# Attention scores of layer 1: the 64-row group taken in two turns of 32 rows

## The chip, the cores and the metric

The kernel runs on one core of a Trainium2 chip. The metric is the device time of one execution, in microseconds. TensorE is called PE (its weight loads PEld), VectorE DVE, ScalarE ACT, GpSimd POOL, and SyncE, which issues most of the DMAs, SP.

## The reference

The program has two layers on an input of 4 x 32 x 128 x 128. Layer 0, a Fourier layer with attention, is not touched. Layer 1 normalizes each token of 128 channels and runs causal additive attention over the 4096 tokens of each of four sequences, then a mixture of eight experts of which each token takes two:

```python
f = jnp.einsum('bih,ha->bia', x, W1[:h])
g = jnp.einsum('bjh,ha->bja', x, W1[h:])
t = jnp.tanh(f[:, :, None, :] + g[:, None, :, :] + b1)
scores = jnp.einsum('bija,a->bij', t, w2[:, 0]) + b2[0]
flag = jnp.tril(jnp.ones((n_seq, n_seq), dtype=x.dtype), -1)[None, :, :]
e = jnp.exp(scores) * flag
denom = jnp.sum(e, axis=-1, keepdims=True) + 1e-10
w = e / denom
return jnp.einsum('bij,bjh->bih', w, x)
```

The score is a sum of 16 terms w2[a] tanh(f + g + b1[a]). All arithmetic is fp32.

## The kernel before

**The scores as products.** A sum of tanh terms over m hidden units can be written as a quotient n / d, where d is a sum over the 2**m patterns of signs of exp(sign sum of the query) times exp(sign sum of the key), and n is the same sum with each pattern weighted by its signed sum of w2. Both are matrix products of a key matrix and a query matrix with 2**m rows. The 16 hidden units are cut into groups of 6, 5 and 5 (`GROUP_SIZES`), so the groups have 64, 32 and 32 rows, 128 together; `_signs` builds the patterns side by side. The score is the sum of the three quotients.

**Keys and queries.** `prepare` makes a chunk of 1024 tokens (`IC`): normalize, transpose, one product each with `mk` and `mq`, then an Exp on ACT. That gives `ke` and `qe` on 128 rows. `ks` is `ke` times the signed sums of w2. `exchange` copies a tile to another with its upper and lower 64 rows swapped, by two DMAs on SP: `kf` from `ks`, `qf` from `qe`. So d is made from `ke` and `qe`, with group 0 on rows 0 to 63 and the others on 64 to 95 and 96 to 127; n is made from `kf` and `qf`, with group 0 on rows 64 to 127 and the others on 0 to 31 and 32 to 63. The helper pieces that do this (`as_keys`, `as_queries`) and those of the expert layer (`attention`, `transpose_half`, `first`, `experts`) are lists of small steps with estimated costs on DVE and POOL; the loop hands out at most one PE piece per unit.

**Units.** A unit is a block of 128 keys against 512 queries (`QC`); there are 528. Units on the diagonal hold two parts of fewer columns. The order is written out by hand (`manual_schedule`), in a loop of stages over u:

- `products(u)` (L1282) on PE: the three products d of unit u and the three products n of unit u-1. They are sorted so that the four products of groups 1 and 2 (32 rows each, on four different row tiles) come first, and then the two of group 0 (64 rows each).
- ACT, L1335: Ln of d into `r`, in two instructions, one on the bank pair of groups 1 and 2 (1024 columns), one on the bank of group 0 (512).
- DVE, L1340: `r` of unit u-1 times n, in the same two parts; then POOL, L1343 and L1344, adds the three groups into `e`, the first two being groups 0 and 1.
- ACT, L1347: Exp of -`r` of unit u (1536 columns), which turns Ln d into 1/d. ACT, L1351: Exp of the score `e` of unit u-2. On diagonal blocks POOL multiplies with the mask `later` (L1356).
- `attend(u-4)` (L1301) on PE: `e` times the normalized tokens `kx`, summed in the bank `po`.
- Then pieces of the other work, above all `experts` (`px`, L1180, with four sums on DVE each, L1184).

**Banks.** The PSUM pool of layer 1 has one buffer per tile. `two_parts` gives d and n a tile of two banks each (`d0`, `n0`: groups 1 and 2) and a tile of one bank each (`d1`, `n1`: group 0); `po` and the pieces' tile `m` have the last two. PE can write a tile of unit u+1 only when ACT (d) or DVE (n) has read that of the unit before.

Of the kernel before, what the change touches and what calls it, by code (L numbers as in the profile page):

```python
# [9 lines left out]
ALU = mybir.AluOpType  # L10
# [3 lines left out]
P = 128  # L14
# [64 lines left out]
def _signs():  # L79


    groups = []
    a = 0
    for m in GROUP_SIZES:
        s = np.zeros((A + 1, 2**m), np.float32)
        for n in range(2**m):
            for i in range(m):
                s[a + i, n] = -1.0 if n >> i & 1 else 1.0
        groups.append(s)
        a += m  # L90
    groups[0][A] = 1.0
    return np.concatenate(groups, 1)


def _inv_std(nc, small, out, var, eps, nhalf):
# [814 lines left out]
def layer1(tc, x1, w1t_in, signs, vec17, expert_w, expert_b, router_w, small_row, out):  # L910
    nc = tc.nc
# [25 lines left out]
        out=later,  # L937
        in_=later,
# [17 lines left out]
    def misc(name):  # L956
# [9 lines left out]
        out=eb.rearrange("p e c -> p (e c)"),  # L966
        in_=expert_b.rearrange("e c -> (e c)").partition_broadcast(P),
    )
    for w, row in (
# [4 lines left out]
        n = w.shape[1]  # L974
# [87 lines left out]
    def prepare(b, i0, own, beside):  # L1062

        kx, ke, kf = own
        xc = work.tile([P, NB, C], F32, name="xc", tag="xc", bufs=4)
        nc.sync.dma_start(out=xc, in_=x1[b, i0 : i0 + NB].rearrange("t w c -> w t c"))
        own_kx = kx[:, i0 : i0 + NB]
        xt = work.tile([P, IC], F32, name="xt", tag="xt", bufs=1)  # L1070
        qe, qf = (work.tile([P, IC], F32, name=n, tag=n, bufs=3) for n in ("qe", "qf"))

        def exchange(dst, src):
            nc.sync.dma_start(out=dst[:64], in_=src[64:])
            nc.sync.dma_start(out=dst[64:], in_=src[:64])

        def as_keys(h):
            i = slice(i0 * P + h * 512, i0 * P + (h + 1) * 512)
            pz = misc("pz")
            nc.tensor.matmul(pz, mk, xt[:, h * 512 : (h + 1) * 512], start=True, stop=True)  # L1080
            nc.scalar.activation(ke[:, i], pz, AF.Exp, bias=kbias)
            ks = work.tile([P, 512], F32, name="ks", tag="ks", bufs=1)
            nc.gpsimd.tensor_scalar(ks, ke[:, i], kmul, None, ALU.mult)
            exchange(kf[:, i], ks)

        def as_queries(h):
            i = slice(h * 512, (h + 1) * 512)
            pz = misc("pz")
            nc.tensor.matmul(pz, mq, xt[:, i], start=True, stop=True)
            nc.scalar.activation(qe[:, i], pz, AF.Exp, bias=qbias)  # L1090
            exchange(qf[:, i], qe[:, i])

        load = [(NONE, 0.0, 0.0, lambda: None), gap] * 2
        sums, after = norm_pieces(xc, own_kx, NB, beside)
        pieces = [(SOME, 0.7, 0.0, lambda h=h: transpose_half(own_kx, xt, h)) for h in range(2)]
        for h in range(2):
            pieces.append((SOME, 0.0, 1.6, lambda h=h: as_keys(h)))
            pieces.append((SOME, 0.0, 0.0, lambda h=h: as_queries(h)))
        return (qe, qf), load + sums + after, pieces
# [125 lines left out]
    state = {}  # L1225
    sums = {}
    live = {}

    def begin(c, beside=True):
# [9 lines left out]
        state[c] = (own, qs)  # L1239
        return norm, pieces  # L1240

    def operands(u, part):


        c, _, _, parts = units[u]
        k, q = state[c][0][1 + part], state[c][1][part]
        for g, r0, n in ((0, 0, 64), (1, 64, 32), (2, 96, 32)):
            r0 = (r0 + 64 * part) % P
            for n_part, (jb, h, q0, c0, c1) in enumerate(parts):
                j = slice(jb * P, (jb + 1) * P)  # L1250
                i = h * QC + q0
                yield g, n_part, c0, c1, k[r0 : r0 + n, j], q[r0 : r0 + n, i : i + c1 - c0]

    PARTS = slice(1, 3), slice(0, 1)

    def two_parts(name):
        return [
            ps.tile([P, g.stop - g.start, 512], F32, name=f"{name}{k}", tag=f"{name}{k}")  # L1260
            for k, g in enumerate(PARTS)
        ]

    def groups_of(parts):
        return parts[1][:, 0], parts[0][:, 0], parts[0][:, 1]

    def products(u):

        todo = []
        if u < len(units):  # L1270
            live[u, "d"] = two_parts("d")
            dst = groups_of(live[u, "d"])
            todo += [(dst[g][:, c0:c1], g, p, k, q) for g, p, c0, c1, k, q in operands(u, 0)]
        if 0 <= u - 1 < len(units):
            live[u - 1, "n"] = two_parts("n")
            dst_n = groups_of(live[u - 1, "n"])
            todo += [
                (dst_n[g][:, c0:c1], g, p, k, q) for g, p, c0, c1, k, q in operands(u - 1, 1)
            ]

        for o, _, _, k, q in sorted(todo, key=lambda t: (t[1] == 0, t[2])):
            nc.tensor.matmul(o, k, q, start=True, stop=True)  # L1282

    kept = []

# [35 lines left out]
    norm_1, todo = begin(1, beside=False)  # L1321
# [6 lines left out]
    with tc.manual_schedule():  # L1328
        for u in range(len(units) + 4):
            products(u)  # L1330
            if u < len(units):
                r = work.tile([P, 3, QC], F32, name="r", tag="r", bufs=3)
                live[u, "r"] = r
                for g, d in zip(PARTS, live.pop((u, "d"))):
                    nc.scalar.activation(r[:, g], d, AF.Ln, scale=1.0 / DSCALE)  # L1335
            if 0 <= u - 1 < len(units):
                v = u - 1
                r, n = live.pop((v, "r")), live.pop((v, "n"))
                for g, part in zip(PARTS, n):
                    nc.vector.tensor_tensor(r[:, g], part, r[:, g], ALU.mult)  # L1340
                e = work.tile([P, QC], F32, name="e", tag="e", bufs=5)
                live[v, "e"] = e
                nc.gpsimd.tensor_tensor(e, r[:, 0], r[:, 1], ALU.add)  # L1343
                nc.gpsimd.tensor_tensor(e, e, r[:, 2], ALU.add)  # L1344
            if u < len(units):
                r = live[u, "r"]
                nc.scalar.activation(r, r, AF.Exp, scale=-1.0)  # L1347
            if 0 <= u - 2 < len(units):
                c, h, _, parts = units[u - 2]
                e = live[u - 2, "e"]  # L1350
                nc.scalar.activation(e, e, AF.Exp)  # L1351
                if parts[0][0] >= chunks[c][1] + h * QB:

                    width = 2 * P if parts[-1][1] != h else P
                    own = e[:, : len(parts) * width].rearrange("p (k c) -> p k c", c=width)[:, :, :P]
                    nc.gpsimd.tensor_tensor(own, own, later[:, : len(parts)], ALU.mult)  # L1356
            if 0 <= u - 4 < len(units):
                attend(u - 4)
                c, h, is_last, _ = units[u - 4]
                if is_last and c == len(chunks) - 1:  # L1360
                    b, i0 = chunks[c]
                    ending.append((b, i0 + h * QB, QB, [sums[c, h]]))
                elif is_last and h == 1:
                    ending.append((*chunks[c], NB, [sums[c, h] for h in range(2)]))

            if starts and u >= starts[0][0] and not todo:
                _, c, end = starts.pop(0)
                todo = sum(begin(c), [])
            if ending and (not ended or len(ended) == 1 and len(ended[0]) <= 2 * NB):
                ended.append(finish(*ending.pop(0)))  # L1370
            hurry = sum(p[0] in (SOME, LATER) for p in todo) + 6 > end - u
            queues = sorted(ended, key=lambda p: len(p) <= 2 * NB)
            queues.insert(0 if hurry else 2, todo)
            pe, dve, pool = False, 0.0, 0.0
            for pieces in queues:
                while pieces:
                    kind, t_dve, t_pool, piece = pieces[0]
                    if kind == LATER:
                        pieces.pop(0)
                        break  # L1380
                    if kind and pe or dve + t_dve > 1.8 or pool and pool + t_pool > 1.7:
                        break
                    if kind in (SOME, KEEPS) and keeper and keeper[0] is not pieces:
                        break
                    pe, dve, pool = pe or kind > 0, dve + t_dve, pool + t_pool
                    if kind in (KEEPS, KEPT):
                        keeper = [pieces] if kind == KEEPS else []
                    pieces.pop(0)
                    piece()
            ended = [p for p in ended if p]  # L1390
# [80 lines left out]
```

## Time and profile before

| | |
|---|---|
| median of 3 runs | 3289.89 us (3287.66 to 3298.04) |
| profiled execution | 3282.17 us, span 3280.4 us, TensorE clock granted 0.971 |
| layer 1's loop | from about 1151 to 3219 us of the span |
| DVE product L1340, 1024 columns | 1.22 us mean; 512 columns 0.68 us |
| POOL add L1343 or L1344 | 1.27 us |
| Exp L1351 | 0.62 us |

The page of the profile lists, for each engine, its busy time, share of the span and number of instructions. A line of a group names the source line, engine, operation, output and inputs, shape and count, then the busy time in us and the mean in ns, then the idle time ahead of it and who ended it. A line of the timeline begins with its start in us from the span's start and its duration. An fp32 product is recorded as two weight loads and two matmuls. `32*128` is the tile shape on TensorE, rows by columns.

### The profile page before, as it was taken

Reading aid. Unit: us, or ns where it says so; the run is one execution under the profiler, and the core shown is the slowest. Engines: PE = TensorE matmul, PEld = TensorE weight load, DVE = VectorE, ACT = ScalarE, POOL = GpSimd, SP = SyncE. Lnnn points to the kernel's source line nnn. Section 1 sums busy time; section 2 is a strip of 40 time slices with the busy share of each in tenths; the row PEclk is TensorE's granted clock in tenths of the full one; section 3 lists DMA queues with packets and bytes.
Section 4 is the critical chain, followed back from the end, with each engine's and each line's share of the span. In section 5 each row is a group of like instructions: output and inputs, shape, how many; then the busy total and the mean of one; then the engine's idle time right before and its main releaser. Section 6 shows DMA issues by size and latency. Waiting matters only on the chain.

```text
span 3280.4 us, 48731 instructions
## 1 busy us (share of the span) xinstructions
PE 3065.3 (93%) x17428; PEld 1488.6 (45%) x17428; DVE 2319.8 (71%) x5070; ACT 2356.6 (72%) x3205; POOL 2138.0 (65%) x1883
## 2 busy tenths in 40 slices
PE   6899899899898699999999999999999999999997
PEld 4378368458558533333333333333333334333333
DVE  6766777767677556777666767766777776677777
ACT  2334444354344289999999999998999999999992
POOL 1730641551460279868798787889877879888773
PEclk8999899999999799999999999999999999999998
DMA  4400510330230111010110000011100010101000
GB/s 109 118 21 1 118 51 1 70 99 1 30 113 1 53 39 26 7 26 7 27 33 20 14 20 14 7 26 26 26 23 11 14 33 20 33 1 26 14 13 13
DMA packets 148274, 107.17 MB, mean 33 GB/s; under 512 B 35358, under 2 KB 138881, under 8 KB 147425
## 3 DMA queue, kind: packets, MB, share of 16 engines
q1 hardware_dynamic: 131313, 98.22, 11.7%
q10 hardware_dynamic: 16720, 5.84, 0.8%
q8 instruction: 138, 2.26, 0.3%
q14 instruction: 103, 0.84, 0.1%
HBM read 67.26 MB, written 20.00 MB: 27 GB/s over the span
## 4 chain that ended last, share of the span: by engine, by line
PE 70%; POOL 12%; DVE 7%; ACT 5%; issue 4%; DMA 2%; ACTq 0%; POOLq 0%; DVEq 0%; SPq 0%
PE d L1282 24%; PE po L1301 12%; PE px L1180 6%; PE po L716 4%; PE pz L272 4%; POOL e L1344 3%; POOL e L1343 3%; PE four L294 3%; PE px L280 2%; PE px L279 2%; PE pv L289 2%; ACT r L1335 2%; POOL kx L1044 2%; PE n L1282 2%; PE sk L680 1%
## 5 line engine op out<-in xcount | busy, mean ns | idle before, releaser
L1282 PE MATMUL d<-qe,ke 32*128 32x512 f32 (+7 forms) x3456 | 1166.2, 603 | 20.9 <-ACT r L1335 20.2
L1340 DVE TENSOR_TENSOR r<-n,r 128x1024 f32<-128x1024 f32 (+1 forms) x1056 | 958.6, 949 | 305.3 <-ACT r L1347 189.0
L1282 PE MATMUL n<-qf,kf 32*128 32x512 f32 (+7 forms) x3456 | 1158.5, 602 | 0.0
L1343 POOL TENSOR_TENSOR e<-r 128x512 f32<-128x512 f32 x528 | 671.9, 1273 | 318.0 <-DVE r L1340 275.8
L1335 ACT ACTIVATE r<-d 128x1024 f32<-128x1024 f32 (+1 forms) x1056 | 823.0, 805 | 69.5 <-PE n L1282 58.8
L1347 ACT ACTIVATE r<-r 128x1536 f32<-128x1536 f32 x528 | 783.4, 1484 | 16.8
L1344 POOL TENSOR_TENSOR e<-e,r 128x512 f32<-128x512 f32 x528 | 671.8, 1272 | 41.4
L1282 PEld LDWEIGHTS d<-qe,ke 32*128 32x128 f32 (+1 forms) x3456 | 351.7, 184 | 701.6 <-issue 239.8
L1301 PE MATMUL po<-e,kx 128*128 128x512 f32 (+3 forms) x1152 | 594.3, 604 | 10.1 <-POOL e L1356 10.1
L1184 DVE SCALAR_TENSOR_TENSOR xc<-px,wgt,xc 128x128 f32<-128x128 f32 x1024 | 358.5, 351 | 211.1 <-PE px L1180 178.5
L1351 ACT ACTIVATE e<-e 128x512 f32<-128x512 f32 x528 | 325.9, 617 | 74.3 <-POOL e L1344 73.9
L1282 PEld LDWEIGHTS n<-qf,kf 32*128 32x128 f32 (+1 forms) x3456 | 350.5, 184 | 19.0 <-DVE r L1340 0.9
L1301 PEld LDWEIGHTS po<-e,kx 128*128 128x128 f32 x1152 | 175.4, 188 | 381.5 <-issue 297.2
L711 POOL TENSOR_TENSOR u<-xb,gb 128x858 f32<-128x858 f32 (+1 forms) x120 | 234.7, 1983 | 118.0 <-PE po L716 93.1
L798 POOL TENSOR_TENSOR spec<-spec,part 128x264 f32<-128x264 f32 x64 | 55.3, 865 | 392.6 <-DVE part L795 187.3
L1180 PE MATMUL px<-we,x2t 128*128 128x512 f32 x512 | 266.3, 606 | 7.1 <-DVE xc L1184 6.2
L713 DVE TENSOR_TENSOR u<-xw,gb 128x858 f32<-128x858 f32 (+1 forms) x200 | 206.9, 1084 | 52.9 <-PE po L716 36.8
L716 PE MATMUL po<-u,pr 128*32 128x429 f32 (+1 forms) x1280 | 188.8, 542 | 18.7 <-POOL u L711 9.0
L705 ACT COPY xw<-xb 128x429 f32<-128x429 f32 (+1 forms) x160 | 83.6, 526 | 122.8 <-DVE pa L557 93.2
L1180 PEld LDWEIGHTS px<-we,x2t 128*128 128x128 f32 x512 | 96.6, 194 | 121.2 <-issue 104.5
L217 ACT COPY z<-pz 128x384 f32<-128x384 f32 x127 | 60.7, 478 | 118.9 <-PE pz L272 118.5
L559 POOL TENSOR_TENSOR pb<-xm 128x1024 f32<-128x1024 f32 x48 | 90.6, 1915 | 81.9 <-ACT xm L493 73.8
(365 smaller groups left out, 3911.2 us busy)
## 6 DMA issues: line engine op xcount, KB each, us to landing
xb<-xd SPq DMA_DIRECT2D x128, 214.5 KB
xc<-x SPq DMA_DIRECT2D x31, 512.0 KB
x<-x SPq DMA_DIRECT2D x16, 512.0 KB
kf<-ks SPq DMA_DIRECT2D x64, 128.0 KB
qf<-qe SPq DMA_DIRECT2D x64, 128.0 KB
out<-xc SPq DMA_DIRECT2D x15, 512.0 KB
xb<-xd SPq DMA_DIRECT2D x32, 198.0 KB
gb<-gd SPq DMA_DIRECT2D x4, 1056.0 KB
```

The costliest lines, as they stand in the source:

```text
L711: nc.gpsimd.tensor_tensor(u, xb, gk, ALU.mult)
L716: nc.tensor.matmul(po[32 * j : 32 * j + 32], pr[:, i, k], u[:, r], start=i == 0 and k == 0, stop=i == 3 and k == 1,)
L1180: nc.tensor.matmul(px, x2t[:, k * P : (k + 1) * P], we[:, e0 : e0 + 4], start=True, stop=True)
L1184: nc.vector.scalar_tensor_tensor(xc[:, k], px[:, e], wgt[:, k, e0 + e : e0 + e + 1], xc[:, k], ALU.mult, ALU.add)
L1282: nc.tensor.matmul(o, k, q, start=True, stop=True)
L1301: nc.tensor.matmul(sums[c, h][:, q0 : q0 + c1 - c0], kx[:, jb], e[:, c0:c1], start=jb == 0, stop=is_last and q0 > 2 * P, skip_group_check= ...
L1335: nc.scalar.activation(r[:, g], d, AF.Ln, scale=1.0 / DSCALE)
L1340: nc.vector.tensor_tensor(r[:, g], part, r[:, g], ALU.mult)
L1343: nc.gpsimd.tensor_tensor(e, r[:, 0], r[:, 1], ALU.add)
L1344: nc.gpsimd.tensor_tensor(e, e, r[:, 2], ALU.add)
L1347: nc.scalar.activation(r, r, AF.Exp, scale=-1.0)
L1351: nc.scalar.activation(e, e, AF.Exp)
```

## The change

The group of 64 rows is multiplied as two products of 32 rows that add up in one bank, the first with start, the second with stop. For d, group 0 is on rows 0 to 31 in both turns and the second group of each turn on rows 32 to 63; for n they are on rows 64 to 95 and 96 to 127. Turn 0 reads `ke` and `qe`, turn 1 `kf` and `qf`, so the columns of `_signs` are put in another order and the tiles hold other halves. `ke` and `kf` now carry both the plain and the weighted keys: three copies of half height per half chunk, the last of which overwrites the lower half of `ke`. The six products of a unit become eight, sorted by part and turn. The tile `d0` now holds groups 1 and 0 and `d1` group 2; `n0` holds groups 0 and 2 and `n1` group 1. POOL first adds groups 0 and 2, then group 1.

```diff
-    return np.concatenate(groups, 1)
+    first, second, third = groups
+    return np.concatenate([first[:, :32], second, first[:, 32:], third], 1)
...
-            exchange(kf[:, i], ks)
+            nc.sync.dma_start(out=kf[:64, i], in_=ke[64:, i])
+            nc.sync.dma_start(out=kf[64:, i], in_=ks[:64])
+            nc.sync.dma_start(out=ke[64:, i], in_=ks[64:])
...
-            exchange(qf[:, i], qe[:, i])
+            nc.sync.dma_start(out=qf[:64, i], in_=qe[64:, i])
+            nc.sync.dma_start(out=qf[64:, i], in_=qe[:64, i])
...
+    ROWS = (((0, 0), (1, 32)), ((0, 0), (2, 32))), (((0, 64), (2, 96)), ((0, 64), (1, 96)))
...
-        k, q = state[c][0][1 + part], state[c][1][part]
-        for g, r0, n in ((0, 0, 64), (1, 64, 32), (2, 96, 32)):
-            r0 = (r0 + 64 * part) % P
+        for turn, rows in enumerate(ROWS[part]):
+            q = state[c][1][turn]
             for n_part, (jb, h, q0, c0, c1) in enumerate(parts):
+                k = state[c][0][1 + turn]
                 j = slice(jb * P, (jb + 1) * P)
                 i = h * QC + q0
-                yield g, n_part, c0, c1, k[r0 : r0 + n, j], q[r0 : r0 + n, i : i + c1 - c0]
+                for g, r0 in rows:
+                    r = slice(r0, r0 + 32)
+                    yield g, (n_part, turn), c0, c1, k[r, j], q[r, i : i + c1 - c0]
...
-    PARTS = slice(1, 3), slice(0, 1)
+    PARTS = {"d": (slice(0, 2), slice(2, 3)), "n": (slice(1, 3), slice(0, 1))}
...
-        for o, _, _, k, q in sorted(todo, key=lambda t: (t[1] == 0, t[2])):
-            nc.tensor.matmul(o, k, q, start=True, stop=True)
+        for o, g, (_, turn), k, q in sorted(todo, key=lambda t: t[2]):
+            nc.tensor.matmul(o, k, q, start=turn == 0 or g > 0, stop=turn == 1 or g > 0)
...
-                nc.gpsimd.tensor_tensor(e, r[:, 0], r[:, 1], ALU.add)
-                nc.gpsimd.tensor_tensor(e, e, r[:, 2], ALU.add)
+                nc.gpsimd.tensor_tensor(e, r[:, 1], r[:, 2], ALU.add)
+                nc.gpsimd.tensor_tensor(e, e, r[:, 0], ALU.add)
```

More of the change, by code (lines that the diff above doesn't have):

```diff
@@ L1071, in prepare @@
         qe, qf = (work.tile([P, IC], F32, name=n, tag=n, bufs=3) for n in ("qe", "qf"))
-        def exchange(dst, src):
-            nc.sync.dma_start(out=dst[:64], in_=src[64:])
-            nc.sync.dma_start(out=dst[64:], in_=src[:64])
         def as_keys(h):
@@ L1260, in two_parts, with groups_of @@
             ps.tile([P, g.stop - g.start, 512], F32, name=f"{name}{k}", tag=f"{name}{k}")
-            for k, g in enumerate(PARTS)
+            for k, g in enumerate(PARTS[name])
         ]
-    def groups_of(parts):
-        return parts[1][:, 0], parts[0][:, 0], parts[0][:, 1]
+    def groups_of(name, parts):
+        places = {}
+        for g, t in zip(PARTS[name], parts):
+            for k in range(g.start, g.stop):
+                places[(1, 0, 2)[k]] = t[:, k - g.start]
+        return places
     def products(u):
@@ L1271, in products @@
             live[u, "d"] = two_parts("d")
-            dst = groups_of(live[u, "d"])
+            dst = groups_of("d", live[u, "d"])
             todo += [(dst[g][:, c0:c1], g, p, k, q) for g, p, c0, c1, k, q in operands(u, 0)]
@@ L1275, in products @@
             live[u - 1, "n"] = two_parts("n")
-            dst_n = groups_of(live[u - 1, "n"])
+            dst_n = groups_of("n", live[u - 1, "n"])
             todo += [
@@ L1333, in layer1 @@
                 live[u, "r"] = r
-                for g, d in zip(PARTS, live.pop((u, "d"))):
+                for g, d in zip(PARTS["d"], live.pop((u, "d"))):
                     nc.scalar.activation(r[:, g], d, AF.Ln, scale=1.0 / DSCALE)
@@ L1338, in layer1 @@
                 r, n = live.pop((v, "r")), live.pop((v, "n"))
-                for g, part in zip(PARTS, n):
+                for g, part in zip(PARTS["n"], n):
                     nc.vector.tensor_tensor(r[:, g], part, r[:, g], ALU.mult)
```

## The prediction

> **What bounds the kernel now.** I read the page first: busy times, then the groups.
>
> ```profile
> PE 3065.3 (93%) x17428; PEld 1488.6 (45%) x17428; DVE 2319.8 (71%) x5070; ACT 2356.6 (72%) x3205; POOL 2138.0 (65%) x1883
> ...
> L1335 ACT ACTIVATE r<-d 128x1024 f32<-128x1024 f32 (+1 forms) x1056 | 823.0, 805 | 69.5 <-PE n L1282 58.8
> L1347 ACT ACTIVATE r<-r 128x1536 f32<-128x1536 f32 x528 | 783.4, 1484 | 16.8
> ```
>
> The change lies in layer 1's attention, 528 units (the count of L1347) from about 1151 us. There PE and ACT are both nearly full, so I went to the order of time. First TensorE alone, in a stretch where one unit has an expert matmul (px) and one has none:
>
> ```profile
> 2510.76 0.70 PE L1282 MATMUL d<-qe,ke 32*128 32x512 f32 x2
> 2510.77 0.70 PE L1282 MATMUL n<-qf,kf 32*128 32x512 f32 x2
> 2511.29 0.59 PE L1282 MATMUL d<-qe,ke 32*128 32x512 f32 x2
> ...
> 2511.83 0.69 PE L1282 MATMUL d<-qe,ke 64*128 64x512 f32 x1
> ...
> 2512.89 1.12 PE L1301 MATMUL po<-e,kx 128*128 128x512 f32 x2
> 2513.85 1.02 PE L1180 MATMUL px<-we,x2t 128*128 128x512 f32 x2
> 2514.80 0.70 PE L1282 MATMUL d<-qe,ke 32*128 32x512 f32 x2
> ```
>
> An fp32 product runs as two passes. Read the starts: four 32-row tiles side by side take 1.07 us, the two 64-row tiles take 1.06, po 0.96, px 0.95. They differ though each has two passes of 512 columns. Weight loads explain it:
>
> ```profile
> 2511.83 0.18 PEld L1282 LDWEIGHTS d<-qe,ke 64*128 64x128 f32 x1 [0.76 <-issue]
> ...
> 2512.89 0.30 PEld L1301 LDWEIGHTS po<-e,kx 128*128 128x128 f32 x2 [0.76 <-issue]
> 2513.43 0.19 PEld L1180 LDWEIGHTS px<-we,x2t 128*128 128x128 f32 x1 [0.24 <-issue]
> ```
>
> px has the tile shape of po. Its weights load at 2513.43, during po's second pass, and it starts at 2513.85, 0.42 after that pass began: one pass streams in about 0.427. Where the shape changes (32 to 64 rows, 64 to 128), the load comes only when the old work is out: 1.07 = 2 x 0.427 + 0.107 (load not hidden) + 0.107 (emptying). A change of shape thus costs about 0.21 us.
>
> Does a second turn on the same 32-row tiles get the cheap hand-over? A unit cut in two parts shows it:
>
> ```profile
> 1359.53 0.91 PE L1282 MATMUL n<-qf,kf 32*128 32x384 f32 x4
> ...
> 1360.27 0.39 PE L1282 MATMUL n<-qf,kf 32*128 32x128 f32 x4
> ```
>
> 384 columns, two passes: 0.107 + 2 x 0.320 = 0.747, so 1360.27. The next product on the same tiles starts with no gap.
>
> Then I took the start-to-start time of the 492 units between 1290.5 and 3213.2 us from the timeline and sorted them by what else PE does in them. Mean 3.908. With px: 4.05 in 207 of 227; with the mean-free attention (pa) or a transpose (pt): 3.63 in 89 of 112; key and query products (pz): 4.05 in 42 of 52; router (pl): 4.87 in all 14; nothing else: 3.19 in 57 of 87. These are exactly PE's own sums (1.07 + 1.06 + 0.96 + 0.95 = 4.04), so PE is the bound in most units. The other 70 or so are longer: 3.43 where ACT sets it, 4.1 to 4.8 where POOL does. ACT's case:
>
> ```profile
> 1637.35 0.70 PE L1282 MATMUL d<-qe,ke 32*128 32x512 f32 x2 [0.18 <-ACT r L1335]
> ...
> 1639.72 1.49 ACT L1335 ACTIVATE r<-d 128x1024 f32<-128x1024 f32 x2
> ...
> 1640.78 0.19 PEld L1282 LDWEIGHTS d<-qe,ke 32*128 32x128 f32 x2 [1.00 <-ACT r L1335]
> ```
>
> A unit's ACT work back to back is 3.43 (1.49 + 1.48 + 0.61 less overlap at the seams); PE restarts 1.06 after the big Ln begins.
>
> **What the Trainium skill says.** "TensorEngine Tiling (Array Packing)", Tiling Modes, Key Properties: changing the tiling mode, not just the tile, drains TensorE. The trace agrees; the price, 0.21 us, is the trace's. "TensorE: Matmul & The Clock Gate", Part 3, The mechanism: a weight load overlaps running matmuls only when the row group differs, though it also names a background weight buffer. Here the same rows' next weights do load during a pass (2513.43 above), so the second half holds. The same page's table of goals says that K=32 takes the time of K=128 and only concurrency gains; the trace agrees, a pass is 0.427 at 32, 64 and 128 rows. "Perfetto Trace Analysis", Tensor Engine Instruction: the matmul end is estimated. So I use starts only.
>
> **The change, part by part.**
> (1) Per unit 6 products become 8, in two rounds of four 32-row tiles. Removed: one round of 64-row tiles (1.06) and one change of shape. Added: a second round with the weights preloaded, 0.854. PE per unit: 0.107 + 4 x 0.427 + 0.107 = 1.92 in place of 2.13. Saving 0.21 on PE, its most over 528 units 112 us. The two extra loads and products run beside the other row tiles.
> (2) The Ln of the two-group bank (1024 columns) now has a group that ends in turn 1. Today it starts 1.17 after the unit's start (the 156 cases where ACT waited for PE), that is 0.21 after the round has streamed. New: 0.107 + 1.708 + 0.21 = 2.03. PE restarts 1.06 later: PE cannot turn over faster than 3.09.
> (3) The same for n: VectorE's 1024 product starts 1.29 after the unit's start where it waited for PE; new 1.29 + 0.85 = 2.14. It frees the bank that turn 0 of the next unit writes: 2.14 + 1.22 (its mean) + about 0.04 (what is left of 1.06 after the Ln's 1.016) = 3.40. Queued behind this product on VectorE are the 512 product and the expert sums of the same unit; the expert sums ahead of it (4 x 0.351) end at about 1.64, before 2.14, so they do not add to it. The first POOL add now waits for one product only; free, since ACT's Exp of e comes some 5 us into the next unit.
> (4) Hence the floor per unit: ACT 3.43, n bank 3.40, d bank 3.09. I take 3.43.
> (5) Keys: three half-height DMAs in place of two, the third (ks to ke) waiting on SP for the first to have read. SP's queue holds later loads of xc and these copies; pieces are planned some 6 units (23 us) ahead, so I cost it at nothing in the loop. In the prologue d now needs the exchanged halves, where d started at 1151.14 before its copies were back; not shown, 0 to 6 us, I take 3.
> (6) The signs' order, POOL's operand order, ranges: nothing, same instructions.
>
> The sum over the 492 units:
> px 213 (207 and six paired with a neighbour): 4.05 to 3.84, -44.7.
> pl 14: -2.9.
> pa and pt 89: 3.63 - 0.21 = 3.42, floor 3.43, so -0.20: -17.8.
> pz 42: ACT has one more Exp (0.67, some 0.59 after overlap), 4.02 alone; the slack of PE against the d loop (3.84 - 3.09) absorbs part of a row of four. Between -0.03 and -0.21, I take -0.12: -5.0.
> none 57: 3.19 to the floor 3.43, +0.24: +13.7. Today ACT may lag behind PE and catch up in the next px unit; the shorter slack takes that away.
> The longer 70-odd: set by POOL or ACT, 0 (bounds -15 to +8).
> Sum -56.7; the 36 units outside at the same mean -4.1; prologue +3. Total -57.8 on the span of 3280.4, or 1.76%. The timed runs have 3287.7 to 3298.0, median 3289.9: 3232.
>
> **Rivals.**
> A, the sum above: 3232, with the bounds of its terms 3210 to 3255. Chance 0.68.
> B, the light units do not meet the floor, and the waiting ones gain too: POOL's adds start after one product, so ACT waits less. For: ACT waits 74 us for POOL's adds on the page. Against: each n bank has one buffer. 112 less 15 to 40: 3178 to 3210, about 3195. Chance 0.14.
> C, the weights of turn 1 are not preloaded, because each of four tiles also waits for a bank: the saving on PE is nil, while the floor costs +13.7 and the prologue +3: 3307. Against: the two-part unit. Chance 0.06. Half of it, only the emptying saved (0.107): 227 x 0.107 = 24, 89 x 0.107 = 10, less 17: about 3274. Chance 0.06.
> D, slower: the n bank's turn-around becomes the bound everywhere. Place: the 1024 product on VectorE, in its order behind expert sums and statistics. A px unit gains nothing once it starts later than 4.05 - 1.26 = 2.79 after the unit's start, against 2.14. If sums plus a pair of statistics end near 3.1, a px unit takes 4.36: 227 x 0.31 = 70, plus 17: 3377, and half of that at 3330. For: VectorE is 71% busy and does these in order. Against: expert sums end at 1.64, and the plan caps pieces at 1.8 us of VectorE per unit. Chance 0.06.
> That the change does not do as said: the diff's rows are (0,32) and (64,96) in both turns, so all shapes are 32*128; no chance of its own.
>
> **Chances and range.** About 0.3%, 10 us, is what a measurement tells from no change. Faster: 0.68 + 0.14 + half of the half case 0.03 = 0.85. Within: 0.04. Slower: 0.11. The range holds A, most of B and A's tail: 3193 to 3264.
>
> **What would show it.** Unit starts at 3.84 with px and near 3.43 for pa and none; the second turn 0.96 after the first, its weight loads 0.43 before it; the big Ln at 2.03 and the big product at 2.14 after the unit's start; L1282's four-tile shapes only. Wrong if px units stay at 4.05 (C), if PE waits for VectorE's r in px units (D), or if none units stay at 3.19 or below (B).

## The result and the profile after

| | before | after |
|---|---|---|
| median, first measurement | 3288.77 us | 3248.61 us, ratio 0.9869 (95% interval 0.9844 to 0.9894) |
| median, second measurement | 3292.96 us | 3245.52 us, ratio 0.9857 (0.9836 to 0.9877) |
| profiled execution, span | 3280.4 us | 3245.1 us |
| layer 1's loop, first unit's start to the last start in the same trace | 2066.1 us (1151.14 to 3217.27) | 2023.3 us (1159.85 to 3183.12) |

The change makes the kernel 1.3 to 1.4% faster. The time is inside the forecast's range and 14 to 17 us above its point of 3232. In the two profiled executions the loop is 42.9 us shorter and what comes after it 1.1. What lies ahead of it is 8.7 us longer, in code that is the same; the last experiment asks whether this is scatter.

The page after, first part and groups:

```profile
PE 3004.3 (93%) x19732; PEld 1584.7 (49%) x19732; DVE 2324.5 (72%) x5070; ACT 2327.1 (72%) x3205; POOL 2138.9 (66%) x1883
...
L1351 DVE TENSOR_TENSOR r<-n,r 128x1024 f32<-128x1024 f32 (+1 forms) x1056 | 961.4, 952 | 481.9 <-PE n L1293 388.5
...
L1346 ACT ACTIVATE r<-d 128x1024 f32<-128x1024 f32 (+1 forms) x1056 | 793.0, 802 | 66.7 <-PE n L1293 59.9
L1358 ACT ACTIVATE r<-r 128x1536 f32<-128x1536 f32 x528 | 783.5, 1484 | 16.7
```

There are 2304 more matmul records, and yet PE is busy 61 us less. DVE's product now waits above all for the n products (388.5 us), which end one turn later. On the page before, its idle time ended most often with ScalarE:

```profile
L1340 DVE TENSOR_TENSOR r<-n,r 128x1024 f32<-128x1024 f32 (+1 forms) x1056 | 958.6, 949 | 305.3 <-ACT r L1347 189.0
```

A unit with an expert product, in order of time (start and duration in us, engine, line, operation):

```profile
2506.73 0.70 PE L1293 MATMUL d<-qe,ke 32*128 32x512 f32 x2
...
2507.26 0.19 PEld L1293 LDWEIGHTS d<-qf,kf 32*128 32x128 f32 x2 [0.23 <-issue]
...
2507.69 0.59 PE L1293 MATMUL d<-qf,kf 32*128 32x512 f32 x2
...
2508.66 1.12 PE L1312 MATMUL po<-e,kx 128*128 128x512 f32 x2
2508.74 1.51 ACT L1346 ACTIVATE r<-d 128x1024 f32<-128x1024 f32 x2 [0.30 <-PE n L1293]
2508.93 1.82 DVE L1351 TENSOR_TENSOR r<-n,r 128x1024 f32<-128x1024 f32 x2 [0.58 <-PE n L1293]
...
2509.62 1.02 PE L1181 MATMUL px<-we,x2t 128*128 128x512 f32 x2
...
2510.57 0.70 PE L1293 MATMUL d<-qe,ke 32*128 32x512 f32 x2
```

Turn 1 starts 0.96 us after turn 0 and its weights load 0.43 before it. From unit to unit it is 3.84, where it was 4.04. The big Ln (1024 columns) starts 2.01 after the unit's start, DVE's product 2.20.

A light unit, with no PE work besides, and the expert unit behind it:

```profile
2590.71 0.70 PE L1293 MATMUL d<-qe,ke 32*128 32x512 f32 x2
...
2592.91 1.82 DVE L1351 TENSOR_TENSOR r<-n,r 128x1024 f32<-128x1024 f32 x2 [0.56 <-PE n L1293]
...
2593.80 0.70 PE L1293 MATMUL d<-qe,ke 32*128 32x512 f32 x2
...
2594.19 0.70 PE L1293 MATMUL n<-qe,ke 32*128 32x512 f32 x2
...
2598.02 0.70 PE L1293 MATMUL d<-qe,ke 32*128 32x512 f32 x2
```

Here the starts of d and n part. d starts again after 3.09, as soon as ACT has read its bank. n starts 0.39 later, 3.47 after the n of the unit before (2590.72): DVE's product of 1024 columns, which began at 2592.91 and takes 1.22 on average, has just ended. As units are counted by the start of d, the delay is booked on the next one, which takes 4.22 instead of 3.84. Below this is called the debt of a light unit.

A transposition that waits for POOL:

```profile
2584.15 1.58 POOL L1046 TENSOR_SCALAR x<-xc,r,mr 128x128 f32<-128x128 f32 x2
...
2585.78 0.33 PE L1061 MATMUL pt<-ident,x 128*128 128x128 f32 x1 [0.38 <-POOL x L1046]
2586.04 0.70 PE L1293 MATMUL d<-qe,ke 32*128 32x512 f32 x2
```

The unit began at 2581.59 and takes 4.45 us. It also holds a second po product; 0.38 of its time is PE's wait for the last normalized block.

All units of the loop by what else PE does in them (count, mean of start to start in us, difference of the sums; worked out from the timelines of both executions). px is an expert product, pa the mean-free attention, pt a transposition, pl the router:

| kind | units | before | after | difference of sums |
|---|---|---|---|---|
| px | 229 | 4.06 | 3.92 | -33.5 |
| none | 102 | 3.44 | 3.50 | +6.5 |
| pa | 62 | 3.67 | 3.56 | -6.4 |
| pt | 60 | 3.87 | 3.83 | -2.1 |
| key and query products | 61 | 4.14 | 4.06 | -5.0 |
| pl | 15 | 4.87 | 4.70 | -2.5 |

### The profile page after: what moved, and what is told of

Read it like the earlier page. It is cut to its first block, busy times and chain, and to the rows that moved or that the text cites. A ratio compares the mean times of both kernels' runs of the same rounds, so it can differ in the third digit from the quotient of the medians.

```text
span 3245.1 us, 53386 instructions
## 1 busy us (share of the span) xinstructions
PE 3004.3 (93%) x19732; PEld 1584.7 (49%) x19732; DVE 2324.5 (72%) x5070; ACT 2327.1 (72%) x3205; POOL 2138.9 (66%) x1883
## 4 chain that ended last, share of the span: by engine, by line
PE 65%; POOL 10%; ACT 9%; DVE 8%; issue 6%; DMA 2%; ACTq 0%; POOLq 0%; DVEq 0%; SPq 0%
PE d L1293 19%; PE po L1312 11%; PE px L1181 6%; ACT r L1346 4%; PE po L718 4%; PE pz L274 4%; PE n L1293 4%; PE four L296 3%; POOL e L1355 3%; PE pv L291 3%; PE px L282 2%; PE px L281 2%; POOL e L1354 2%; ACT e L1362 2%; PE sk L682 1%
## 5 line engine op out<-in xcount | busy, mean ns | idle before, releaser
L1351 DVE TENSOR_TENSOR r<-n,r 128x1024 f32<-128x1024 f32 (+1 forms) x1056 | 961.4, 952 | 481.9 <-PE n L1293 388.5
L1346 ACT ACTIVATE r<-d 128x1024 f32<-128x1024 f32 (+1 forms) x1056 | 793.0, 802 | 66.7 <-PE n L1293 59.9
L1293 PE MATMUL d<-qe,ke 32*128 32x512 f32 (+3 forms) x2304 | 611.0, 605 | 38.2 <-ACT r L1346 36.3
L1293 PE MATMUL n<-qe,ke 32*128 32x512 f32 (+3 forms) x2304 | 608.4, 603 | 0.0
L1293 PE MATMUL d<-qf,kf 32*128 32x512 f32 (+3 forms) x2304 | 555.2, 556 | 0.0
L1293 PE MATMUL n<-qf,kf 32*128 32x512 f32 (+3 forms) x2304 | 555.0, 556 | 0.0
L1293 PEld LDWEIGHTS d<-qe,ke 32*128 32x128 f32 x2304 | 177.6, 184 | 360.1 <-ACT r L1346 340.8
L1293 PEld LDWEIGHTS d<-qf,kf 32*128 32x128 f32 x2304 | 221.8, 187 | 177.1 <-issue 164.5
L1293 PEld LDWEIGHTS n<-qf,kf 32*128 32x128 f32 x2304 | 229.0, 186 | 20.0 <-issue 12.4
L1293 PEld LDWEIGHTS n<-qe,ke 32*128 32x128 f32 x2304 | 178.0, 183 | 9.8 <-DVE r L1351 0.9
```

Source lines behind the costliest of these rows:

```text
L1293: nc.tensor.matmul(o, k, q, start=turn == 0 or g > 0, stop=turn == 1 or g > 0)
```

## The experiments

The theory after the result: the saving on PE is as forecast. Three things hold part of it back. The n bank's turn-around (the time until its next product can be written) keeps light units from gaining; POOL takes back part at transpositions; ScalarE's work is a floor beside both. The rivals are that only one of these matters.

**po between the turns.**

```diff
-        for o, g, (_, turn), k, q in sorted(todo, key=lambda t: t[2]):
+        done = False
+        for o, g, (n_part, turn), k, q in sorted(todo, key=lambda t: t[2]):
+            if turn and not done:
+                done = True
+                between()
...
-            products(u)
+            products(u, lambda: attend(u - 4) if 0 <= u - 4 < len(units) else None)
```

> The changed kernel with the product po (unit u-4) placed between turn 0 and turn 1. Nothing is added; an expert unit gets four changes of tile shape instead of two, and the last n product ends 1.28 us later after the unit's start. Theory (floors from the banks' turn-around): big Ln at 2.03 + 1.28 = 3.31, d loop 4.37; VectorE's 1024 product at 2.20 + 1.28 = 3.48, n loop 3.48 + 1.22 + 0.04 = 4.74. All kinds of unit lie near 4.74, the loop at some 530 x 4.75 = 2518 us, in all about 3740. Rival 1 (only TensorE's sum counts, a shape change 0.21): expert units 3.84 + 0.43 = 4.27, light ones 3.09 as before, in all about 3345. Rival 2 (the d loop alone): 4.37 everywhere, about 3545.

One execution took 3741.26 us against 3740 expected. From the chip's timeline of this kernel:

```profile
2541.48 0.70 PE L1297 MATMUL d<-qe,ke 32*128 32x512 f32 x2
2541.86 0.70 PE L1297 MATMUL n<-qe,ke 32*128 32x512 f32 x2
2542.92 1.12 PE L1318 MATMUL po<-e,kx 128*128 128x512 f32 x2
2543.98 0.70 PE L1297 MATMUL d<-qf,kf 32*128 32x512 f32 x2
2545.32 1.82 DVE L1357 TENSOR_TENSOR r<-n,r 128x1024 f32<-128x1024 f32 x2 [2.91 <-PE n L1297]
2546.60 0.70 PE L1297 MATMUL n<-qe,ke 32*128 32x512 f32 x2
```

The product on DVE starts 3.46 after n, n comes back after 4.74, and the mean from one Exp of `r` to the next is 4.75. Of all 527 such steps 388 round to 4.7. So the bank's turn-around (last n, 0.37 to the product, 1.22 for it, 0.06 to PE) is the rule, and PE's sum alone, or the d bank alone, is not. po and turn 1 are 1.06 apart, as the two products of 64 rows were before, with a change of shape on both sides; po followed by px of the same shape took 0.96.

**n in three one-bank tiles.**

```diff
-    PARTS = {"d": (slice(0, 2), slice(2, 3)), "n": (slice(1, 3), slice(0, 1))}
+    PARTS = {"d": (slice(0, 2), slice(2, 3)), "n": (slice(2, 3), slice(1, 2), slice(0, 1))}
```

> The changed kernel with the tile of n's groups 0 and 2 cut in two one-bank tiles; VectorE multiplies group 2 first (512 columns), then 0, then 1. Theory (the n bank's turn-around, 3.47 us from unit to unit, is what keeps light units from gaining): group 2's bank is free at 1.33 + 0.68 = 2.01 and group 0's at 2.20 + 0.68 = 2.88 after the unit's start, so the floor is ScalarE's 3.43 on average and the d bank's 3.09 for a single unit. A unit with no other TensorE work after an expert unit takes 3.09 and the expert unit behind it 3.84 instead of about 4.20: some 25 places x 0.36 = 9 us less than the changed kernel, about 3240, ratio to before 0.985. Rival (the floor is ScalarE's work alone): expert units behind a light one stay at 4.20, 3249, ratio 0.988.

Measured 3240.06 us, ratio 0.9839 (0.9815 to 0.9863); the loop takes 2016.2, 7.1 less than in the first trace of the changed kernel. Its timeline:

```profile
2595.48 1.48 ACT L1358 ACTIVATE r<-r 128x1536 f32<-128x1536 f32 x1
...
2597.05 1.89 DVE L1351 TENSOR_TENSOR r<-n,r 128x512 f32<-128x512 f32 x3 [0.52 <-PE n L1293]
...
2809.87 0.70 PE L1293 MATMUL d<-qe,ke 32*128 32x512 f32 x2
...
2812.97 0.59 PE L1293 MATMUL d<-qe,ke 32*128 32x384 f32 x2
2812.98 0.70 PE L1293 MATMUL n<-qe,ke 32*128 32x512 f32 x2
...
2816.81 0.70 PE L1293 MATMUL d<-qe,ke 32*128 32x512 f32 x2
```

d and n start together again, and the unit behind the light one takes 3.84. The 34 expert units directly behind a light one have a median of 3.85, where the changed kernel has 4.18. One step of the expectation was wrong: the first product starts 2.04 after its unit's start (2595.01), not 1.33. The trace names PE, but that product also needs Exp of r, which ends at 2596.96, 0.09 before it. The bank comes free at 2.04 + 1.25 for the two products that matter = 3.29, instead of 2.20 + 1.22 = 3.42. The times of the whole kernels overlap in their scatter. The rival is refuted by the 34 units, and by the loop, which differs by only 1.2 us between two traces of the changed kernel.

**The Exp of the scores left out, without and with the three tiles.**

```diff
-                nc.scalar.activation(e, e, AF.Exp)
```

> The changed kernel with the Exp of the scores left out (the attention uses raw scores), so that ScalarE has 0.6 us less per unit, 2.83 in place of 3.43. Theory (the n bank's turn-around of 3.47 is a floor of its own beside ScalarE's): attention units stay at 3.43 to 3.47 and pairs of light units at a mean of 3.47; a light unit may start d at 3.09 and has the rest booked on the unit behind it. Rival (ScalarE's work is the floor): attention units at 3.42 all, light units at 3.09 with no debt.

> The same (the Exp of the scores left out) and n in three one-bank tiles. Theory: both upper floors are gone, and the d bank's 3.09 is left: light units 3.09 in a row, expert units 3.84 also behind light ones, attention units 3.42. Rival (another floor near 3.4, such as VectorE's order): light units in a row stay at 3.4.

One execution each: 3234.30 and 3212.53 us; loops 2014.0 and 1998.7. Without Exp alone, attention units stay at 3.43 and 3.46 in turn, and 29 of the 34 expert units behind light ones take 3.97 to 4.25: the n bank is a floor of its own. With both, attention units take 3.43, which is PE's sum, and light ones come in rows of 3.15:

```profile
2713.80 0.70 PE L1293 MATMUL d<-qe,ke 32*128 32x512 f32 x2
...
2716.95 0.70 PE L1293 MATMUL d<-qe,ke 32*128 32x512 f32 x2
...
2720.11 0.48 PE L1293 MATMUL d<-qe,ke 32*128 32x256 f32 x2
```

So ScalarE's 3.43 and the n bank's 3.47 lie one on the other, and taking both away gives more than the two alone together (24.6 us, against 9.3 and 7.1). The expectation was met in part only: light units stop at 3.15 and not 3.09, and the expert units behind them have a median of 3.95 and not 3.84, so some debt is left. Neither is explained.

**The normalization's last step moved to VectorE,** in the changed kernel, in the kernel before, and beside the three tiles.

```diff
-                engine.tensor_scalar(
+                nc.vector.tensor_scalar(
                     dst[:, k], src[:, k], r[:, k : k + 1], mr[:, k : k + 1], ALU.mult, ALU.subtract
```

> The changed kernel with the last step of the normalization (the scale and shift of each 128 x 128 block) on VectorE instead of GpSimd inside the loop; the plan of pieces is the same. Theory (part of TensorE's saving is given back where transposes and masked units wait for GpSimd): units with transposes go from a mean of 3.83 to about 3.5 (60 x 0.33 = 20 us), light units at 4.1 come down too; 20 to 30 us less than the changed kernel, about 3224, ratio to before 0.980. Rival (GpSimd is off the path, the loss at transposes is TensorE's and the bank's own): 3249 or a little more, since VectorE gets 0.27 us per block more ahead of its product.

> The kernel before with the same move of the normalization's last step to VectorE. Theory (GpSimd took back part of the change's gain): the kernel before waits less at transposes (60 x 0.24 = 14 us over TensorE's sum of 3.63) and in masked units, so it gains 15 to 20, about 3272, ratio 0.995; the difference between this one and the changed kernel with the same move is then about 48 us, more than the 40 without it. Rival (GpSimd waits cost both alike): both gain the same and the difference stays at 40.

> The changed kernel with both edits: n in three one-bank tiles, and the normalization's last step on VectorE. Theory: the two gains add, 9 and 25 us: about 3215, ratio to before 0.978. Rival (VectorE becomes the bound, since it gets 0.14 us more per unit and the blocks): no better than the better of the two alone, 3224 or more.

All three missed: 3378.75 us (ratio 1.0248, 1.0224 to 1.0273), 3387.19 (1.0285, 1.0262 to 1.0308) and 3373.91 (1.0243, 1.0219 to 1.0267). The instructions of that line, with minimum, median and maximum in ns, first in the kernel before:

```profile
L1044 POOL TENSOR_SCALAR kx<-xc,r,mr x112: 777/793/816, 1205.7 to 2955.1; 128x128 f32<-128x128 f32 x112
L1044 DVE TENSOR_SCALAR kx<-xc,r,mr x16: 328/340/711, 1138.8 to 1148.5; 128x128 f32<-128x128 f32 x16
```

and in the changed kernel with the move:

```profile
L1046 DVE TENSOR_SCALAR kx<-xc,r,mr x128: 327/919/1430, 1153.8 to 3035.4; 128x128 f32<-128x128 f32 x128
L1046 DVE TENSOR_SCALAR x<-xc,r,mr x128: 331/1283/1446, 1256.3 to 3352.6; 128x128 f32<-128x128 f32 x128
```

The expectation took VectorE's price from the prologue, where POOL is idle: 0.34. In the loop, beside POOL's adds, the same instruction has a median of 0.92 for `kx` and 1.28 for `x`, longer than POOL needs for it. The Trainium skill, "Trainium Architecture — The Big Picture", What this means for kernel authors, says that VectorE and GpSimd share a pair of SBUF ports under an exclusive lock. The trace agrees: 203 of the 256 blocks take over 0.6 us, and 202 of these end 0.07 to 0.10 us after a POOL instruction does, nearly always one of the adds. The 35 blocks that meet no POOL instruction take 0.33 to 0.34. So these runs do not show how much POOL's waits cost.

**POOL's second add left out,** in both kernels.

```diff
-                nc.gpsimd.tensor_tensor(e, e, r[:, 0], ALU.add)
```

> The changed kernel without GpSimd's second add per unit (the term of group 1 is left out of the score), 1.27 us less of GpSimd's 3.2 us per unit. Theory (part of TensorE's saving is given back to waits for GpSimd): layer 1's loop falls from 2023 to what the other floors give, expert units 229 x 3.84, light 102 x 3.45, attention 62 x 3.45, transposes 60 x 3.46, key and query 61 x 3.87, router 15 x 4.67: about 1960 to 1975. Rival (GpSimd is off the path): about 2023.

> The kernel before, likewise without the second add (the term of group 2 is left out). Theory: its loop falls from 2066 to 2024 to 2035 (229 x 4.05, 102 x 3.27, 62 x 3.63, 60 x 3.63, 61 x 4.05, 15 x 4.87), so that the change is worth 55 to 64 us in the loop without GpSimd in the way, against 43 with it, near the 61 of the forecast's sum. Rival (GpSimd costs both kernels the same, or nothing): the difference stays at 43.

The changed kernel came to 3190.75 us (ratio 0.9690, 0.9663 to 0.9717), the kernel before to 3242.23 (0.9844, 0.9817 to 0.9871). The loops take 1968.6 and 2022.1. POOL's load on the page of the changed kernel without the add (it was 2138.9 us with it):

```profile
PE 2989.7 (94%) x19732; PEld 1594.6 (50%) x19732; DVE 2323.6 (73%) x5070; ACT 2319.0 (73%) x3205; POOL 1477.2 (46%) x1355
```

With POOL relieved the change is worth 53.6 us in the loop, without that 42.9. This is a little under the 55 to 64 expected, well over the rival's 43. The kinds say where: pa and pt together gain 8.5 + 8.9 = 17.4 between the two kernels without the add, and 6.4 + 2.1 = 8.5 between the kernels themselves (4.0 with the second trace of the changed one). Key and query products gain 10.1 in place of 5.0; light units lose 12.1 in place of 6.5. PE's own waits for POOL in the two whole kernels, from 1400 to 3180 us (total in us, times, longest), first before, then after:

```profile
PE po L1301 <- POOL e L1356: 8.1, 10, 1.9
PE pt L1059 <- POOL x L1044: 1.4, 4, 0.4
PE pt L1059 <- POOL kx L1044: 1.2, 4, 0.4
...
PE po L1312 <- POOL e L1367: 11.1, 9, 2.1
PE pt L1061 <- POOL x L1046: 2.6, 6, 0.5
PE pt L1061 <- POOL kx L1046: 1.7, 4, 0.5
```

They grow from 10.7 to 15.4 us, and most of them stand ahead of po, where POOL's mask on diagonal blocks comes late, not at the transpositions. The two edits are not quite alike: without the second add, `e` needs only VectorE's first product in the changed kernel, but both products in the kernel before. From 1200 to 3120 us of their traces, though, no product on PE and no Exp of `e` on ScalarE waits for POOL any more, so this does not set them apart. Leaving the add out saves 44.0 us of the loop in the kernel before and 54.7 in the changed one, more than the change itself brings.

**The step moved to ScalarE instead,** with the three tiles.

```diff
-            engine.tensor_scalar(mr[:, v], mr[:, v], 1.0, None, ALU.subtract)
+            engine.tensor_scalar(mr[:, v], mr[:, v], -1.0, 1.0, ALU.mult, ALU.add)
...
-                engine.tensor_scalar(
-                    dst[:, k], src[:, k], r[:, k : k + 1], mr[:, k : k + 1], ALU.mult, ALU.subtract
-                )
+                nc.scalar.activation(
+                    dst[:, k], src[:, k], AF.Identity, bias=mr[:, k : k + 1], scale=r[:, k : k + 1]
+                )
```

> The changed kernel with n in three one-bank tiles and the normalization's scale and shift (128 x 128 blocks) on ScalarE instead of GpSimd. ScalarE gets some 0.3 us per block (from 0.617 at 512 and 1.016 at 1024 columns), 0.6 per piece, so 4.03 in a unit with a piece, and such units mostly alternate with others. Theory (GpSimd's waits are worth 20 us or more and ScalarE has the room beside expert units): 10 to 20 us under the kernel with three tiles alone, about 3225, ratio to before 0.980. Rival (ScalarE's floor rises and takes it back): 3240 to 3260.

Measured 3234.31 us, ratio 0.9829 (0.9807 to 0.9851), between the theory and the rival, and not told apart from the three tiles alone. Its price row:

```profile
L1046 ACT ACTIVATE kx<-xc,mr,r x128: 477/479/493, 1140.9 to 2912.9; 128x128 f32<-128x128 f32 x128
```

A block costs 0.48, not 0.3, so a unit with a piece has 3.43 + 0.96 on ScalarE. Transpositions fall to 3.79 on average (3.92 with three tiles alone), and light units rise to 3.57 (3.50). This is the fastest of the full kernels by its median, by less than its interval.

**The changed kernel once more.**

> The changed kernel once more, for the place of the difference: the profiled execution of it spent 8.7 us more than that of the kernel before ahead of layer 1's first product, in code that is the same. Theory (that is scatter between executions): layer 1's loop takes 2023 us again, within 2, and what lies ahead of it moves by several us either way. Rival (the change moves layer 0 through the placement of its buffers or code): layer 0 is longer by 8 to 9 us again.

The loop takes 2024.5 us, 1.2 from the first trace. The first unit starts at 1158.70, again 7.6 later than in the first trace of the kernel before, as the rival had it. But layer 0 is the same in all executions here, and over them the first unit starts anywhere from 1150.1 to 1166.2, with the old layer 1 at 1151.1, 1155.8 and 1158.7. The old ones lie inside the range of the new ones, so the 8.7 us ahead of the loop in the first pair of traces can be scatter; a shift of the mean by a few us is not excluded by three executions of the old one.

## Why the prediction was right, and where its sum was off

**One change of shape less per unit, 0.21 us.** Right. Expert units went from 4.05 to 3.84, the weights of turn 1 loaded 0.43 ahead, and turn 1 followed after 0.96. For px the forecast had -44.7. The sum shows -33.5, but 34 expert units stand behind a light one and carry its debt. In the kernel with three tiles these units have a mean of 3.94, against 4.16, which is 7.7 us in all; without that px has -41.2. Rival C is out.

**The floors.** The d bank's 3.09 was exact (2590.71 to 2593.80). The n bank's was 3.40 and measured 3.47: VectorE starts its product 2.20 after the unit's start, not 2.14; why the forecast's 1.29 + 0.85 is 0.06 short is not shown. This put the n bank above ScalarE's 3.43, which the forecast had taken for all. Light units: +13.7 forecast; +6.5 on them and the 7.7 behind them, some 14. Rival B is out: light units met the floor, even though 3.09 stands on many of them, since the rest is booked on the next. Rival D did not come in expert units, where the product mostly starts at 2.20, well before 2.79.

**Attention and transposition units.** This term was mis-sized: -17.8 forecast, -8.5 measured (-4.0 with the second trace). The forecast set the units that wait for POOL at nothing and let all the others reach the floor. But some units that had not waited do so now: three transposition units of 3.62 became 4.38, and three others that were long already grew by 0.6 to 0.7. Without POOL's second add the same kinds gain 17.4, so POOL's part is shown. That faster expert units bring these pieces sooner to a POOL that is no faster is the likely reason, but only argued.

**The sum in the loop.** The forecast was -60.8, the measurement -42.9. Of the 17.9 between them, 11.2 are missing at px (7.7 of it debt), 9.3 at attention and transposition units, 0.4 at the router, and 4.1 are the forecast for units outside its 492, which the table has in its kinds. Light units cost 7.2 less than forecast on their own account. Relieving POOL brings back 10.7 of the 17.9.

**Keys, queries, router.** -5.0 and -2.9 forecast, -5.0 and -2.5 measured. The first agreement is partly luck: without POOL's second add the key and query units gain 10.1, so POOL, which the forecast had not counted there, also holds them back.

**The prologue.** +3 forecast. From the last product on the expert weights to the first unit it is 23.2 us in both traces. The first two units, which need the exchanged halves first, take 13.8 in place of 13.0, so the start costs some 0.7.

## What to carry to other kernels

On TensorE, count the changes of tile shape per step, not only the passes: here products of one shape next to each other preloaded their weights, and one change was worth 0.21 us. Where two turns write one bank, work out how soon each reader can free it, per bank; here a floor that only light steps met was paid in part by the steps behind them. And where a change speeds up the bound engine, look at the engines that feed its rarer work: here POOL's waits left 42.9 us of a gain of 53.6.

## What the runs showed of the hardware that was not expected

- VectorE's scale and shift of a 128 x 128 fp32 block in SBUF takes 0.34 us with GpSimd idle and a median of 0.92 (`kx`) or 1.28 (`x`) beside GpSimd's adds, mostly ending just after an add does; moving 240 such blocks off GpSimd made both kernels 2.5 to 2.9% slower.
- The weights of a second product on the very same 32 rows load while the first one streams (2507.26), also with four row tiles side by side.
- ScalarE's Identity with scale and bias per partition takes 0.48 us for 128 columns, against 0.617 for an Exp of 512 without them.
